# Local attention of a fused transformer: averages feature-major, two tiles projected at once, inverse norms by logarithm and exponential, another order within a period

## The chip, the cores and the metric

The kernel runs on one core of a Trainium2 chip. The metric is the device time of one execution in microseconds; the median of several runs is compared. A profiled execution gives the engine-by-engine record that the prediction works from. Engines are called as in the profile: PE (matrix products, with PEld for its weight loads), DVE (vector engine), ACT (scalar engine), POOL (GpSimd) and SP (the queue that issues most DMAs).

## The reference

Four sequences of 512 tokens with 128 features pass through four stages, each a cross-attention and a feed-forward part. The change concerns one of them only, the feed-forward part of the third stage, which is itself a transformer of six layers with local attention (16 heads of 64 features, windows of 32 tokens). Cut to what matters:

```python
def l2norm(t):
    return t / jnp.maximum(jnp.linalg.norm(t, axis=-1, keepdims=True), 1e-12)

def attn_layer(x, Wqkv, qs, ksc, Wo):
    qkv = x @ Wqkv
    q, k, v = (sh(t) for t in jnp.split(qkv, 3, -1))     # 16 heads of 64
    q = l2norm(q) * qs
    k = l2norm(k) * ksc
    q = q * cos * scale + rotate_half(q) * sin * scale
    k = k * cos * inv + rotate_half(k) * sin * inv
    # each window of 32 queries sees its own window and the one before it
    sim = jnp.einsum('bhwie,bhwje->bhwij', bq, bk2) * QK_SCALE
    sim = jnp.where(mask, -jnp.finfo(sim.dtype).max, sim)
    attn = jax.nn.softmax(sim, -1)
    out = jnp.einsum('bhwij,bhwje->bhwie', attn, bv2)
    return out.transpose(0, 2, 1, 3).reshape(b, n, INNER) @ Wo

def ffn_layer(x, g, bln, W1, b1, W2, b2):
    xn = (x - mu) / jnp.sqrt(var + 1e-05) * g + bln
    a, gate = jnp.split(xn @ W1 + b1, 2, -1)
    return a * jax.nn.gelu(gate, approximate=False) @ W2 + b2

for i in range(6):
    x = attn_layer(shift_tokens(x), Wqkv[i], q_scale[i], k_scale[i], Wo[i]) + x
    x = ffn_layer(shift_tokens(x), ln_g[i], ln_b[i], W1[i], b1[i], W2[i], b2[i]) + x
```

`shift_tokens` delays the second half of the features by one token.

## The kernel before, in words

Everything here happens in `local_transformer`. The residual stream is held feature-major in `Y[b]` (128 features by 512 tokens and one column more, so that the shift by a token is an offset of one column for partitions 64 to 127). The work on one **tile** is that on 128 tokens of one sequence in one layer: 6 layers x 4 sequences x 4 tiles = 96 tiles. A **row** is the four tiles of one sequence in one layer; its feed-forward part comes after all four.

One loop over `n` issues one **period** at a time. A period holds steps of three tiles at different ages and of one row:

- `T`, tile n: products for queries and keys (`queries_or_keys`, two halves `c` of eight heads for each `kind`: 0 queries, 1 keys), squares on ACT (L1781), the rotation on DVE (`rotate`: two products, L1789 and L1792, and the sum of squares, L1801), their sum on POOL (L1802), the inverse norms (`normalise`: a first guess by integer arithmetic on DVE, L1812 and L1813, then three Newton steps, L1817 to L1820, and the scaling, L1823, all on POOL), and the values (`values`, L1858, copied by ACT, L1859, and shifted by a window into `v2` by DMAs of SP's queue, L1861 to L1869).
- `T1`, tile n-1: queries and keys are transposed (`turned`, with `to_features`, L582; ACT copies, L1835; POOL copies the last 32 keys of the tile before in front, L1831), the scores (L1879 the mask, L1888), and the softmax up to the exponential (L1898 maximum, L1899 difference, L1904 exponential).
- `T2`, tile n-2: the probabilities are transposed (L582, ACT copies L1909), the averages (`average`, L1919), their division by the sum that a column of ones in V yields (`normalised`, L1928 and L1929), the transposition to features (`attended`, ACT copies L1938), the projection (L1943) and the residual (L1950).
- `F`, a row: its feed-forward part in four **phases**, one to a period. Phase 0: `ff_moments` early, `ff_norm` late. Phase 1: `ff_turn` early, `ff_gate` of chunks 0 and 1 (Gelu, L1981) late. Phase 2: `ff_gate` of chunk 2 early, `ff_up` (L1989, L1992) of chunks 0 and 1 late. Phase 3: `ff_up` of chunk 2 early, `ff_down` (L2001) and its residual (L1716) late. The phase of a period equals the place of T2 in its row.

There is no scheduler in this part: each engine works through its instructions in the order in which the loop issues them, and waits by semaphore for what others must have done. [...] two for `mm` (products for queries and keys), two for `tr` (all transposes, and the values), a pair `sc` (scores, and all of the feed-forward part) and a pair `av` (averages and projection).

## Time and profile before

| | |
|---|---|
| median of 3 runs | 2536.09 us (2535.72 to 2539.29) |
| profiled execution | 2544.82 us, of which the span from the first to the last instruction is 2543.0 us |
| mean granted PE clock | 0.944; 1.00 in the stretch from 700 to 2215 us |
| busy share of the span | PE 90%, PEld 59%, DVE 70%, ACT 49%, POOL 61% |
| local transformer | maximum of the softmax (L1898) 96 times, first at 568.6 us, last at 2209.6 us |
| from one maximum to the next | 17.54, 17.10, 18.39 and 15.65 us in turn where a feed-forward part runs beside; 15.17 us in the first tiles, where none does |

A row of the timeline gives the start in us, the duration, the engine, the line, the operation, what it writes and reads with its shape, how many are merged, and in brackets how long the engine was idle before and what ended that. A matmul of 32-bit floats appears as two instructions, its two passes, each with a weight load. Since the ends of matmuls are modelled, the distance from start to start is what a product costs in a stream. A group's row gives the busy total and the mean of one in ns, then the idle time of the engine before the group and its releasers. A row of waits reads: who waited for whom, us in total, times, longest. A row of a stretch gives the busy time and count for PE, PEld, DVE, ACT and POOL, then the clock, the DMA share and GB/s.

### The profile page before, as it was taken

How to read it: one execution, taken by the hardware profiler on the slowest of the kernel's cores; microseconds unless marked ns; L12 is line 12 of the kernel's file. 1: busy time of each engine (PE TensorE's matmuls, PEld its weight loads, DVE VectorE, ACT ScalarE, POOL GpSimd, SP SyncE). 2: the span in 40 equal slices, each digit the busy share in tenths (PEclk: the TensorE clock that was granted, in tenths of full speed). 3: DMA queues.
4: the chain of work that ended last, by engine and by line, in shares of the span. 5: the costliest groups of instructions: out<-in, count | busy, mean ns of one | idle time of the engine just before them, and what ended most of it. 6: DMA issues, size and time to landing. Idle time of an engine off the chain costs nothing.

```text
span 2543.0 us, 87670 instructions
## 1 busy us (share of the span) xinstructions
PE 2287.4 (90%) x37341; PEld 1489.2 (59%) x37341; DVE 1789.3 (70%) x4010; ACT 1245.4 (49%) x2186; POOL 1549.6 (61%) x2620
## 2 busy tenths in 40 slices
PE   7959879968999999999999999999999999878676
PEld 3537744536666666666666666666666666634465
DVE  5436355757888888888888888788888888646422
ACT  3523234535555555555555555555555555514232
POOL 2241232447777777777777777777777777532333
PEclk9868989979999999999999999999999999969788
DMA  6201110015311121111211121111211111102023
GB/s 160 82 20 40 37 41 2 1 49 110 105 28 34 33 61 43 32 28 34 75 28 34 34 71 34 32 28 47 60 29 34 33 27 34 28 27 58 19 70 85
DMA packets 134305, 116.21 MB, mean 46 GB/s; under 512 B 29505, under 2 KB 102700, under 8 KB 133916
## 3 DMA queue, kind: packets, MB, share of 16 engines
q1 hardware_dynamic: 128373, 102.81, 15.5%
q0 software_dynamic: 4608, 7.35, 0.9%
q8 instruction: 296, 4.85, 0.8%
q14 instruction: 93, 0.76, 0.1%
q10 hardware_dynamic: 935, 0.43, 0.1%
HBM read 42.84 MB, written 21.52 MB: 25 GB/s over the span
## 4 chain that ended last, share of the span: by engine, by line
PE 54%; DVE 24%; issue 7%; ACT 6%; POOL 4%; DMA 2%; another core or an unknown queue 1%; SPq 1%; ACTq 0%; POOLq 0%; DVEq 0%
PE ps_tr L582 8%; PE ps_mm L1779 8%; DVE rc L1789 4%; DVE rs L1792 4%; DVE ss L1801 4%; PE ps_av L1919 3%; PE ps_av L1943 3%; PE ps_tr L1858 3%; PE ps_sc L1989 3%; PE ps_sc L2001 3%; PE ps_sc L1888 2%; DVE P L1899 2%; PE ps L773 2%; DVE la_mx L1898 2%; PE ps L782 2%
## 5 line engine op out<-in xcount | busy, mean ns | idle before, releaser
L1802 POOL TENSOR_TENSOR rc<-rc,rs 128x512 f32<-128x512 f32 x384 | 488.4, 1275 | 229.3 <-DVE rs L1792 187.6
L1779 PE MATMUL ps_mm<-wqk,y 128*128 128x512 f32 x768 | 397.7, 600 | 11.0 <-DVE rs L1792 7.6
L1823 POOL TENSOR_TENSOR rc<-rc,rn_y 128x512 f32<-128x512 f32 x384 | 388.8, 1044 | 7.5
L1789 DVE TENSOR_TENSOR rc<-ps_mm,tabs 128x512 f32<-128x512 f32 x384 | 262.5, 684 | 163.0 <-ACT sq L1781 147.6
L1904 ACT ACTIVATE P<-P 128x1024 f32<-128x1024 f32 x96 | 101.5, 1057 | 419.8 <-DVE P L1899 419.8
L1781 ACT ACTIVATE sq<-ps_mm 128x512 f32<-128x512 f32 x384 | 231.0, 602 | 150.5 <-PE ps_mm L1779 103.0
L1792 DVE TENSOR_TENSOR rs<-ps_mm,tabs 128x512 f32<-128x512 f32 x384 | 261.6, 681 | 5.8 <-POOL rc L1802 5.7
L1801 DVE TENSOR_REDUCE ss<-sq 128x8 f32<-128x512 f32 x384 | 259.5, 676 | 0.0
L582 PE MATMUL ps_tr<-cst,rc 128*128 128x128 f32 x1536 | 211.4, 281 | 8.7 <-POOL rc L1823 4.5
L1919 PEld LDWEIGHTS ps_av<-v,PT 64*32 64x32 f32 x12288 | 138.0, 105 | 126.7 <-PE ps_tr L582 55.0
L1943 PE MATMUL ps_av<-aT,wo 128*128 128x128 f32 x1536 | 199.0, 282 | 4.5 <-issue 4.4
L1943 PEld LDWEIGHTS ps_av<-aT,wo 128*128 128x128 f32 x1536 | 180.8, 193 | 13.5 <-issue 4.7
L582 PEld LDWEIGHTS ps_tr<-cst,rc 128*128 128x128 f32 x1536 | 165.6, 141 | 28.7 <-POOL rc L1823 5.6
L1919 PE MATMUL ps_av<-v,PT 64*32 64x65 f32 x12288 | 169.1, 225 | 6.4 <-DVE attn L1929 5.9
L1017 POOL DMA_INDIRECT back<-ye,to x80 | 78.0, 975 | 157.5 <-DVE ye L1131 111.9
L1888 PE MATMUL ps_sc<-kT,qT 64*32 64x64 f32 x12288 | 146.4, 225 | 30.0 <-issue 22.6
L1888 PEld LDWEIGHTS ps_sc<-kT,qT 64*32 64x32 f32 x12288 | 139.8, 105 | 40.9 <-issue 27.0
L1779 PEld LDWEIGHTS ps_mm<-wqk,y 128*128 128x128 f32 x768 | 124.9, 193 | 61.0 <-issue 45.0
L763 ACT ACTIVATE P<-ps,deltaT 77x512 f32<-77x512 f32 x192 | 115.4, 683 | 73.6 <-PE ps L757 68.3
L1835 ACT COPY kT<-ps_tr 128x512 f32<-128x512 f32 x192 | 103.3, 589 | 86.1 <-PE ps_tr L582 84.9
L1835 ACT COPY qT<-ps_tr 128x512 f32<-128x512 f32 x192 | 103.2, 589 | 74.8 <-PE ps_tr L582 72.4
L1929 DVE TENSOR_TENSOR attn<-ps_av,la_den 128x512 f32<-128x512 f32 x192 | 132.8, 691 | 6.6
(392 smaller groups left out, 4510.8 us busy)
## 6 DMA issues: line engine op xcount, KB each, us to landing
v<-v SPq DMA_DIRECT2D x432, 65.0 KB
v<-v SPq DMA_DIRECT2D x96, 195.0 KB
wqk<-in_L_ffn_Wqkv_dram SPq DMA_DIRECT2D x24, 256.0 KB
sent<-xn SPq DMA_DIRECT2D x2, 2210.0 KB
xe<-sent SPq DMA_DIRECT2D x16, 260.0 KB
back<-xn SPq DMA_DIRECT2D x2, 2048.0 KB
raw<-in_L_ffn_W_dram SPq DMA_DIRECT2D x8, 512.0 KB
yb<-back SPq DMA_DIRECT2D x16, 256.0 KB
```

What stands on the lines that cost most here:

```text
L582: PE.transpose(t[:, i], src[:, i], ident)
L1779: PE.matmul(t, lhs, T.w[2 * kind + c], start=True, stop=True)
L1781: SC.activation(sq, t, AF.Square)
L1789: V.tensor_tensor(a, t, bc(T.tabs[:, 2 * kind, tt], [128, 8, LD], 1), ALU.mult)
L1792: V.tensor_tensor(r.rearrange("p h (x d) -> p h x d", x=2), t.rearrange("p h (x d) -> p h x d", x=2)[:, :, ::-1], bc(T.tabs[:, 2 * kind + ...
L1801: V.tensor_reduce(T.ss[:, kind, 8 * c : 8 * c + 8], sq, AX.X, ALU.add)
L1802: G.tensor_tensor(a, a, r, ALU.add)
L1823: G.tensor_tensor(a, a, bc(y[:, o : o + 8], [128, 8, LD], 2), ALU.mult)
L1835: SC.copy(t[:, 4 * c : 4 * c + 4, lead:], to_features(T.rot[kind, c].rearrange("p (k x) d -> p k (x d)", x=2)),)
L1888: PE.matmul(T.banks[32 * w : 32 * w + 32, z, k], T.qT[r, k, 32 * w : 32 * w + 32], T.kT[r, k, 32 * w : 32 * w + 64], start=False, stop=Tru ...
L1919: PE.matmul(T.means[32 * w : 32 * w + 32, x0, k], T.PT[r, 4 * g + k, 32 * w : 32 * w + 32], (T.v1 if w % 2 else T.v2)[r, x0, 4 * g + k], s ...
L1943: PE.matmul(t, T.wo[:, c], T.aT[:, c], start=(c == 0), stop=(c == 7))
```

## The change

- The probabilities are divided by their sums before the averages: `sums` (DVE: sum and reciprocal over the exponentials) and `shares` (POOL: two products, in place). V loses its column of ones, `normalised` goes.
- `average` takes V as the stationary operand (64 rows by 64 columns) and the transposed probabilities as the moving one (32 columns), and writes the means of all eight head pairs feature-major into the pair `av`. `attended` copies them without a transpose, into a buffer that holds two tiles.
- `project_out` and `residual` run in the periods whose T2 is the second or fourth of its row, for two tiles, 256 columns.
- `normalise` finds the inverse norms as exp(-0.5 ln(ss)) on ACT with one Newton step on POOL, which also takes the first step over from DVE. The table set that holds both functions is loaded explicitly before the loop and after the last Gelu of each row.
- The sum of `rotate` becomes a step of its own, `added`; the scaling becomes `scaled`, for queries in the same period and for keys in the next.
- The steps of a period are issued in another order.

```diff
+EXP_LN = "natural_log_exp_and_others"
...
@@ -1799,6 +1800,10 @@
                     ALU.mult,
                 )
                 V.tensor_reduce(T.ss[:, kind, 8 * c : 8 * c + 8], sq, AX.X, ALU.add)
+                T.rot[kind, c] = a, r
+
+            def added(T, kind, c):
+                a, r = T.rot[kind, c]
                 G.tensor_tensor(a, a, r, ALU.add)
                 T.rot[kind, c] = a
 
@@ -1809,18 +1814,19 @@
                 ss = T.ss.rearrange("p a b -> p (a b)")
                 y = small.tile([128, n], F32, name="rn_y")
                 t = small.tile([128, n], F32, name="rn_t")
-                V.tensor_scalar(ss, ss, 1e-24, -0.5, ALU.max, ALU.mult)
-                V.tensor_scalar(
-                    y.bitcast(I32), ss.bitcast(I32), -0.5, 0x5F3759DF - 0x40400000, ALU.mult, ALU.add
-                )
-                for _ in range(3):
-                    G.tensor_tensor(t, y, y, ALU.mult)
-                    G.tensor_tensor(t, t, ss, ALU.mult)
-                    G.tensor_scalar(t, t, 1.5, None, ALU.add)
-                    G.tensor_tensor(y, y, t, ALU.mult)
-                for (kind, c), a in sorted(T.rot.items()):
-                    o = LH * kind + 8 * c
-                    G.tensor_tensor(a, a, bc(y[:, o : o + 8], [128, 8, LD], 2), ALU.mult)
+                G.tensor_scalar(ss, ss, 1e-24, -0.5, ALU.max, ALU.mult)
+                SC.activation(y, ss, AF.Ln, scale=-2.0)
+                SC.activation(y, y, AF.Exp, scale=-0.5)
+                G.tensor_tensor(t, y, y, ALU.mult)
+                G.tensor_tensor(t, t, ss, ALU.mult)
+                G.tensor_scalar(t, t, 1.5, None, ALU.add)
+                G.tensor_tensor(y, y, t, ALU.mult)
+                T.inverse = y
+
+            def scaled(T, kind):
+                for c in range(2):
+                    a, o = T.rot[kind, c], LH * kind + 8 * c
+                    G.tensor_tensor(a, a, bc(T.inverse[:, o : o + 8], [128, 8, LD], 2), ALU.mult)
 
             def turned(T, kind):
 
@@ -1844,19 +1850,17 @@
             def values(T, x0):
 
 
-
                 b, tt = T.b, T.tt
                 if x0 == 0:
-                    T.v1 = vp.tile([128, 2, LH // 2, LD + 1], F32, name="v1")
-                    T.v2 = vp.tile([128, 2, LH // 2, LD + 1], F32, name="v2")
-                    G.memset(T.v1[:, :, :, LD : LD + 1], 1.0)
+                    T.v1 = vp.tile([128, 2, LH // 2, LD], F32, name="v1")
+                    T.v2 = vp.tile([128, 2, LH // 2, LD], F32, name="v2")
                     if tt == 0:
                         G.memset(T.v2[0:32, 0], 0.0)
                         G.memset(T.v2[64:96, 1], 0.0)
                 t = p_tr(128, 8, LD)
                 src = Y[b] if x0 == 0 else swapped[b]
                 PE.matmul(t, src[:, 128 * tt : 128 * tt + 128], T.wv[:, x0], start=True, stop=True)
-                SC.copy(T.v1[:, x0, :, 0:LD], t)
+                SC.copy(T.v1[:, x0], t)
                 if x0 == 0:
                     DMA.dma_start(T.v2[32:128, 0], T.v1[0:96, 0])
                     if tt:
@@ -1893,60 +1897,69 @@
 
             def softmax(T):
 
-                P = tp.tile([128, LH // 2, 2, LD], F32, name="P", bufs=1)
+                T.P = tp.tile([128, LH // 2, 2, LD], F32, name="P", bufs=1)
+                P = T.P.rearrange("p k z d -> p z k d")
                 mx = small.tile([128, 2, LH // 2], F32, name="la_mx")
                 V.tensor_reduce(mx, T.banks, AX.X, ALU.max)
-                V.tensor_tensor(
-                    P.rearrange("p k z d -> p z k d"), T.banks,
-                    bc(mx, [128, 2, LH // 2, LD], 3), ALU.subtract,
-                )
-                T.P = P.rearrange("p k z d -> p k (z d)")
+                V.tensor_tensor(P, T.banks, bc(mx, [128, 2, LH // 2, LD], 3), ALU.subtract)
                 SC.activation(T.P, T.P, AF.Exp, scale=8.0)
+
+            def sums(T):
+                T.sum = small.tile([128, LH // 2, 2], F32, name="la_sum")
+                V.tensor_reduce(T.sum, T.P, AX.X, ALU.add)
+                V.reciprocal(T.sum, T.sum)
+
+            def shares(T):
+
+                for g in range(2):
+                    k = slice(4 * g, 4 * g + 4)
+                    P = T.P[:, k].rearrange("p k z d -> p (k z) d")
+                    rec = T.sum[:, k].rearrange("p k z -> p (k z)")
+                    G.tensor_tensor(P, P, bc(rec, [128, 8, LD], 2), ALU.mult)
 
             def probabilities(T):
                 T.PT = tp.tile([128, LH // 2, 128], F32, name="PT", bufs=1)
+                P = T.P.rearrange("p k z d -> p k (z d)")
                 for g in range(2):
-                    SC.copy(T.PT[:, 4 * g : 4 * g + 4], to_features(T.P[:, 4 * g : 4 * g + 4]))
-
-            def average(T, g):
-                if g == 0:
-                    T.attn = tp.tile([128, LH // 2, 2, LD], F32, name="attn", bufs=1)
-                T.means = pair("av")[:, :, : 4 * LD + 4].rearrange("p x (k d) -> p x k d", d=LD + 1)
-                for k in range(4):
+                    SC.copy(T.PT[:, 4 * g : 4 * g + 4], to_features(P[:, 4 * g : 4 * g + 4]))
+
+            def average(T):
+
+
+                t = pair("av").rearrange("p s (k q) -> p s k q", q=64)
+                for k in range(LH // 2):
                     for w in range(4):
                         for x0 in range(2):
                             r = slice(64 * (x0 ^ (w // 2)), 64 * (x0 ^ (w // 2)) + 64)
+                            q = 32 * (w % 2)
                             PE.matmul(
-                                T.means[32 * w : 32 * w + 32, x0, k],
-                                T.PT[r, 4 * g + k, 32 * w : 32 * w + 32],
-                                (T.v1 if w % 2 else T.v2)[r, x0, 4 * g + k],
-                                start=True, stop=True,
+                                t[64 * x0 : 64 * x0 + 64, w // 2, k, q : q + 32],
+                                (T.v1 if w % 2 else T.v2)[r, x0, k],
+                                T.PT[r, k, 32 * w : 32 * w + 32], start=True, stop=True,
                             )
-
-            def normalised(T, g):
-                den = small.tile([128, 2, 4], F32, name="la_den")
-                V.reciprocal(den, T.means[:, :, :, LD])
-                V.tensor_tensor(
-                    T.attn[:, 4 * g : 4 * g + 4].rearrange("p k x d -> p x k d"),
-                    T.means[:, :, :, 0:LD], bc(den, [128, 2, 4, LD], 3), ALU.mult,
-                )
+                T.means = t
 
             def attended(T):
-                flat = T.attn.rearrange("p k x d -> p k (x d)")
-                T.aT = tp.tile([128, LH // 2, 128], F32, name="aT", bufs=1)
-                for g in range(2):
-                    SC.copy(T.aT[:, 4 * g : 4 * g + 4], to_features(flat[:, 4 * g : 4 * g + 4]))
+
+                if T.tt % 2 == 0:
+                    T.aT = tp.tile([128, LH // 2, 256], F32, name="aT", bufs=1)
+                else:
+                    T.aT = T.before.aT
+                for s in range(2):
+                    o = 128 * (T.tt % 2) + 64 * s
+                    SC.copy(T.aT[:, :, o : o + 64], T.means[:, s])
 
             def project_out(T):
-                t = pair("av")[:, 0, :128]
+
+                t = pair("av")[:, 0, :256]
                 for c in range(8):
                     PE.matmul(t, T.wo[:, c], T.aT[:, c], start=(c == 0), stop=(c == 7))
                 T.out = t
 
             def residual(T):
-                t = T.out
-                for r, o in ((slice(0, 64), 0), (slice(64, 128), 1)):
-                    dst = Y[T.b][r, 128 * T.tt + o : 128 * T.tt + o + 128]
+                t, o0 = T.out, 128 * (T.tt - 1)
+                for r, o in ((slice(0, 64), o0), (slice(64, 128), o0 + 1)):
+                    dst = Y[T.b][r, o : o + 256]
                     V.tensor_tensor(dst, t[r], dst, ALU.add)
 
 
@@ -2020,6 +2033,7 @@
                     ff_up(F, 0, 1)
                 elif phase == 2:
                     ff_gate(F, 2)
+                    SC.preload_act_table_set(EXP_LN)
                 elif phase == 3:
                     ff_down(F) if second else ff_up(F, 2)
 
@@ -2030,6 +2044,7 @@
             loaded = {0: load(0)}
             tabs = {0: tables(loaded[0][5])}
             swap(0)
+            SC.preload_act_table_set(EXP_LN)
             for n in range(len(tiles) + 10):
                 T = tiles[n] if n < len(tiles) else None
                 T1 = tiles[n - 1] if 0 <= n - 1 < len(tiles) else None
@@ -2051,32 +2066,36 @@
                     T.tabs = tabs[T.i]
                     queries_or_keys(T, 0, 0)
                 if T2:
-                    probabilities(T2)
+                    sums(T2)
                 if T:
                     queries_or_keys(T, 0, 1)
                     rotate(T, 0, 0)
+                if T1:
+                    scaled(T1, 1)
+                if T2:
+                    shares(T2)
+                if T1:
+                    turned(T1, 0)
                 if F:
                     ff_stage(F, phase, False)
-                if T2:
-                    average(T2, 0)
-                if T1:
-                    turned(T1, 0)
                 if T:
+                    added(T, 0, 0)
                     queries_or_keys(T, 1, 0)
-                if T2:
-                    normalised(T2, 0)
-                if T:
                     rotate(T, 0, 1)
-                if T2:
-                    average(T2, 1)
+                    added(T, 0, 1)
                 if T1:
                     turned(T1, 1)
+                if T2:
+                    probabilities(T2)
                 if T:
+                    rotate(T, 1, 0)
+                    added(T, 1, 0)
                     queries_or_keys(T, 1, 1)
                 if T2:
-                    normalised(T2, 1)
+                    average(T2)
                 if T:
-                    rotate(T, 1, 0)
+                    rotate(T, 1, 1)
+                    added(T, 1, 1)
                 if T2:
                     attended(T2)
                 if T and T.tt == NT - 1 and n + 1 < len(tiles):
@@ -2084,12 +2103,11 @@
                 if T1:
                     scores(T1)
                 if T:
-                    rotate(T, 1, 1)
-                if T:
                     normalise(T)
+                    scaled(T, 0)
                 if T1:
                     softmax(T1)
-                if T2:
+                if T2 and T2.tt % 2:
                     project_out(T2)
                     residual(T2)
                 if F and phase == 0:
```

## The prediction

> **What bounds the kernel now.** I read the page's first two parts, then busy time by stretch, the totals of waits, the groups, and last the timeline of one engine at a time. The local transformer owns two thirds of the span: the first maximum of its softmax (L1898) starts at 568.6 us and the last at 2209.6. The page and a stretch inside it:
>
> ```profile
> PE 2287.4 (90%) x37341; PEld 1489.2 (59%) x37341; DVE 1789.3 (70%) x4010; ACT 1245.4 (49%) x2186; POOL 1549.6 (61%) x2620
> ```
>
> ```profile
> 1100.00:1500.00 400.00, 384.68 (x7740) 257.93 (x7739) 332.15 (x612) 227.62 (x391) 308.56 (x538) 1.00 0.14 38
> ```
>
> PE shows 96% busy at clock 1.00, but its ends are modelled, so I count starts. Without feed-forward work a tile needs 14.13 us of PE (602.25 to 616.4, start to start), yet L1898 comes every 15.17 us there (568.56, 583.66, 598.83, 614.00). So PE is not the first bound. The waits say what is:
>
> ```profile
> ACT P L1904 <- DVE P L1899: 419.8, 96, 6.0
> POOL rc L1802 <- DVE rs L1792: 187.6, 244, 6.0
> DVE rc L1789 <- ACT sq L1781: 147.6, 54, 5.7
> ```
>
> DVE and ACT wait for each other in a ring. One turn, from phase 1 to phase 2 of a row, on DVE and then on ACT:
>
> ```profile
> 1431.54 1.22 DVE L1898 TENSOR_REDUCE la_mx<-ps_sc 128x16 f32<-128x1024 f32 x1
> 1432.79 1.23 DVE L1899 TENSOR_TENSOR P<-ps_sc,la_mx 128x1024 f32<-128x1024 f32 x1
> ...
> 1439.17 0.69 DVE L1789 TENSOR_TENSOR rc<-ps_mm,tabs 128x512 f32<-128x512 f32 x1 [4.65 <-ACT sq L1781]
> ```
>
> ```profile
> 1434.05 1.06 ACT L1904 ACTIVATE P<-P 128x1024 f32<-128x1024 f32 x1 [4.10 <-DVE P L1899]
> 1435.02 1.06 ACT L1859 COPY v<-ps_tr 128x512 f32<-128x512 f32 x2
> 1436.09 1.28 ACT L1981 ACT_TABLE_LOAD   x1
> 1437.38 1.27 ACT L1981 ACTIVATE fh<-ps_sc,cols 128x512 f32<-128x512 f32 x2
> 1438.54 0.60 ACT L1781 ACTIVATE sq<-ps_mm 128x512 f32<-128x512 f32 x1
> ```
>
> Maximum, difference, exponential, V copies, in this phase table and Gelu, then the squares that the first rotation waits for. From 1439.17 DVE is solid to the next maximum at 1449.08: four rotations of 1.80, two normalisations of 0.83, 1.0 for L1812 and L1813. The intervals between maxima repeat as 17.54, 17.10, 18.39, 15.65: **68.68 us a row** of four tiles, in which PE has 4 x 14.13 + 8.85 of feed-forward = 65.4.
>
> [...] 105 ns at 32 columns and 193 at 128 is 0.92 ns a column. [...] the trace has 1283 ns for each switch and two switches a row, and keeps two.
>
> **Part by part, per tile.**
>
> ```profile
> L1802 POOL TENSOR_TENSOR rc<-rc,rs 128x512 f32<-128x512 f32 x384 | 488.4, 1275 | 229.3 <-DVE rs L1792 187.6 <-PE ps_tr L582 36.1 <-PE ps_sc L1956 2.0
> L1823 POOL TENSOR_TENSOR rc<-rc,rn_y 128x512 f32<-128x512 f32 x384 | 388.8, 1044 | 7.5
> L1919 PEld LDWEIGHTS ps_av<-v,PT 64*32 64x32 f32 x12288 | 138.0, 105 | 126.7 <-PE ps_tr L582 55.0 <-PE ps_mm L1779 22.1 <-ACT PT L1909 21.3
> L1943 PEld LDWEIGHTS ps_av<-aT,wo 128*128 128x128 f32 x1536 | 180.8, 193 | 13.5 <-issue 4.7
> ```
>
> - DVE: out go two L1929 and L1928 (1.66) and L1812, L1813 (1.0). In come a sum over 1024 elements (1.25, as L1898) and a reciprocal (0.2). The residual, four 64x128 per two tiles at 0.285, becomes two 64x256 (0.42, as L2110): -0.15. Net -1.35.
> - POOL: twelve Newton steps (4.1) become five (1.7); dividing P adds two of L1823's form (2.0); a memset goes (0.1). Net -0.5, but POOL now waits for Ln and Exp on ACT: 128x32, 0.23 each as L917, with hand-overs 0.65. Net about zero.
> - ACT: +0.46 for these two, in a queue 57% busy. The copies stay 512 wide.
> - PE: 8 transposes of the average go (0.97 with the mode change behind them, of which 0.1 returns between average and scores). The projection was 16 passes at 118 ns (1.89); two tiles together take 16 passes of 256, 0.216 each by half of a 512 pass (0.43), 3.46 for two: -0.16.
> - The average stays 128 passes, moving 32 columns instead of 65, loading 64 instead of 32. Today they start 10.2 ns apart (64 in 0.65 us). **No trace row has 64x64**: below, today's pace, 1.3 us; [...] I take 1.7 plus 0.1 drain; today 1.6 plus 0.3 drains.
>
> PE's own work falls to 13.1 a tile, 61.3 a row. Memsets of v2, V's DMAs (65 columns to 64) and their SP queue keep their places; the averages read V two periods later, and that distance hides them, so I cost them at nothing; were it gone, the four issues of about 0.56 us on SP's queue, 2.2 us a tile.
>
> **The walk.** Work is not the bound, so I lay the new order out engine by engine, in order, with these durations; hand-overs from the timeline: PE start to ACT 1.11 (a 512 product), squares to rotation 0.63, rotation to POOL's sum 1.42. Zero is the first product of phase 0.
>
> Phase 0: DVE still has the residual of ff_down (to 1.74), and now `sums` before the first rotation: 3.2 instead of 1.75. POOL divides P 3.3 to 5.3, then stands at the feed-forward's inverse deviation, now queued before `added`; it needs the moments (6.07) and ends 7.5. Behind it wait two sums and the kT head, to 10.4, for which scores wait: 10.5 to 12.15. Maximum 12.35, difference to 14.85, exponential 15.95, V copies, squares, next rotation 17.45. PE's phase ends at 13.9 for 11.9 of work. POOL ends Ln, Exp, Newton and `scaled` of queries at 17.3.
>
> Phase 1: so turning the queries waits until 17.4 (PE was free 15.6), POOL scales keys to 19.3 and divides P to 21.35; probabilities are turned 21.4, fourth product, average 23.25, scores 25.05, the double projection 26.7 to 30.15, values 31.9. V copies, table and Gelu lie behind values: squares 35.15, rotation 35.8. PE's phase ends 33.6.
>
> Phase 2: the preload follows Gelu in ACT's queue (38.0 to 39.3). Squares, kT and PT copies stand behind it; the two transpose banks are full, and PE turns probabilities only from 40.35. Average 42.3, scores 44.1 to 45.75. No projection covers the softmax here, so ff_up waits for the score banks until 48.45; DVE gets both chunks at 50.45 and ends 51.85.
>
> Phase 3: `sums` to 53.3, rotation, ff_up's chunk, rotation; probabilities 57.8, average 58.75, scores 60.55, projection 62.2, values 65.65, ff_down 67.4 to **70.0**.
>
> A row is 70.0 against 68.68, the gain of the DVE ring being spent on POOL's longer queue, the preload and two bunched projections: +1.3 x 24 = +32 us. About 7 tiles without feed-forward gain 0.85 each (POOL near 14.3 against 15.17): -6. New tables every layer (3 us on POOL) cost as now. Sum +26 on the profiled execution's 2544.8 (span 2543.0), 2570.8; the median of the runs is 8.7 lower: **2562 us**.
>
> **Rivals.**
> 1. *Faster: POOL and the preload do not hold PE.* Place: turning queries and probabilities in phases 1 and 2. If the waits there vanish, PE's 61.3 plus the 3.3 a row that it loses today is 64.6: -4.1 x 24 - 6 = -104, 2432 us. For it: POOL waits 229 us today before L1802, room for dividing; the DVE ring is 2 us shorter. Against: dividing sits ahead of the sums in an ordered queue. It decides once probabilities are turned within about 0.5 us of PE being free; half the effect, and an average at today's pace (-0.4 in three phases, -29 us), give 2485. I expect 2430 to 2530.
> 2. *Much slower: the average's loads are not hidden.* 20 ns a pass, +0.9 in phases 1, 2 and 3: +65, 2627 us. [...] Against: 128-column passes of L773 start four at a time every 110 ns, with no room for a load in turn.
> 3. *No change:* 2536, if gains and waits cancel. That the new normalisation changes nothing by itself, POOL net zero, speaks for it.
>
> **Chances.** Under 0.2% (5 us) no measurement of this kernel tells. The walk 0.43, own range 2545 to 2605 (0.6 us a row and the average between its lower bound and mine); rival 2 0.15; rival 1 0.36; rival 3 0.06. Slower 0.58, same 0.06, faster 0.36. The range 2470 to 2630 leaves out the lower part of rival 1 and the tail of rival 2, 0.2 together.
>
> **What would show it.** In the changed profile: no L1929 form and fewer transposes; averages of 128 passes in 1.7 us; ACT waiting for POOL before Ln; PE's transposes of P waiting for POOL in phase 1 and for ACT's copies in phase 2; ff_up's product waiting for DVE's difference; intervals of maxima near 14.5, 19, 16.5 and 20. I am wrong if the sum of four falls under 67, or if PE starts its average without such waits; and in size if the average takes under 1.4 or over 2.3.

## The result, and the profile after

The changed kernel takes **2834.71 us** in the median of 4 runs (2825.08 to 2851.57), the kernel before beside it 2537.50 (4 runs). The ratio is 1.117, with a 95% interval of 1.114 to 1.121: slower by 297 us, where 26 were forecast. The profiled execution took 2828.35 us, with a span of 2826.6.

The page's engine line and the row of the same stretch as before (busy time of PE, PEld, DVE, ACT, POOL, each with its count, then clock, DMA share, GB/s):

```profile
PE 2280.1 (81%) x35805; PEld 1462.2 (52%) x35805; DVE 1691.9 (60%) x3530; ACT 1299.4 (46%) x2379; POOL 1566.6 (55%) x2044
```

```profile
1100.00:1500.00 400.00, 327.49 (x6244) 214.90 (x6237) 259.36 (x417) 203.29 (x371) 269.24 (x348) 0.99 0.13 33
```

All five engines lost share in the stretch (PE 384.7 to 327.5, DVE 332.2 to 259.4). No engine has become a bound by its work; each now waits for others. The local part, first to last maximum, went from 1641.1 us to 1936.6: 295.5 us, nearly all of the difference. The totals of waits name the place (waiting engine and line, the one it waits for: us, times, longest). After:

```profile
DVE la_mx L1903 <- PE ps_sc L1892: 334.3, 96, 13.3
...
POOL P L1918 <- DVE la_sum L1910: 310.9, 77, 18.7
...
PEld ps_sc L1892 <- issue: 172.0, 97, 4.8
...
PE ps_sc L1892 <- issue: 156.6, 96, 4.6
...
PEld ps_mm L1780 <- DVE rs L1793: 138.6, 95, 8.9
...
PE ps_av L1935 <- issue: 27.6, 33, 5.8
```

And the rows of before that answer to the third and the first:

```profile
PEld ps_sc L1888 <- issue: 27.0, 27, 1.5
...
DVE la_mx L1898 <- PE ps_sc L1888: 3.9, 3, 3.0
```

Before, the maximum waited for scores in 3 tiles of 96, 3.9 us in all. Now it does in every tile, 334.3 us. The scores' weight loads stood 27.0 us without a releaser ("issue"), now 172.0. And PE's products for queries and keys wait 95 times for a rotation, 94 of them the third product of a tile; before, they did so 3 times. POOL, which the prediction made the narrow place, waits for DVE's sums.

The chain of waits through one tile (start, us, what). It is read downwards; each line was released by the one above:

```profile
1382.56 0.61 DVE rs L1793
1383.21 1.14 PE ps_mm L1780 x2
1384.43 0.60 ACT sq L1782
1385.03 0.48 ACT kT L1841
1385.64 1.12 PE ps_tr L583 x8
1386.76 0.86 PE ps_mm L1780 x2
1387.62 1.98 PE ps_av L1935 x119
1389.60 0.71 issue
1390.31 0.42 PE ps_av L1935 x9
1391.08 1.12 PE ps_sc L1892 x76
1392.20 1.58 issue
1393.78 0.43 PE ps_sc L1892 x17
1394.24 1.24 DVE la_mx L1903
```

A rotation frees one of the two PSUM buffers `mm` for the third product; then follow the key copy, the transposes of P, the fourth product, average, scores, maximum, and from there the sums and the next rotation. It is a closed ring: in the same trace the rotation after this maximum ends at 1401.1 us, and the next third product starts at 1401.17. Of one turn 11 us run on PE and ACT, while DVE has only three rotations and, in this phase, the statistics of a layer norm left to do. DVE shows the end of them and the gap:

```profile
1389.93 0.68 DVE L1802 TENSOR_REDUCE ss<-sq 128x8 f32<-128x512 f32 x1
1394.24 1.22 DVE L1903 TENSOR_REDUCE la_mx<-ps_sc 128x16 f32<-128x1024 f32 x1 [3.63 <-PE ps_sc L1892]
```

Two lines of that chain are "issue": the profile shows nothing that PE waited for, and yet it did nothing. PE's timeline of the same tile shows where:

```profile
1387.55 2.05 PE L1935 MATMUL ps_av<-PT,v 64*64 64x32 f32 x119
1390.31 0.42 PE L1935 MATMUL ps_av<-PT,v 64*64 64x32 f32 x9 [0.71 <-issue]
1390.67 0.41 PE L1883 MATMUL ps_sc<-maskw,identb 64*32 64x512 bf16 x8
1390.89 1.31 PE L1892 MATMUL ps_sc<-kT,qT 64*32 64x64 f32 x111
1393.78 0.35 PE L1892 MATMUL ps_sc<-kT,qT 64*32 64x64 f32 x17 [1.58 <-issue]
```

From stall to stall there are 9 + 8 + 111 = 128 passes, with their weight loads 256 instructions. The block stalls twice, each time by more than 0.4 us, in 30 of the 96 tiles, and in all 30 the distance is exactly 128 passes. The page's row of the instruction queue (packets, MB, share) fits that:

```profile
q8 instruction: 284, 4.65, 0.7%
```

4.65 MB in 284 packets is 16.4 kB a packet. How much of PE's work goes with one is shown by the runs: the kernel with half of the average, below, has 12,288 fewer instructions on PE and PEld (2 x 29,661 against 2 x 35,805) and 48 fewer packets (236), the kernel before 3,072 more (2 x 37,341) and 12 more packets (296). That is 256 instructions a packet both times, 64 bytes each, and 256 is the distance of the stalls. In the dense stretch above two such transfers start at 1387.30 and 1391.44 us, 4.1 us apart; in the whole trace no two start less than 3.2 us apart (theory F, below, puts this at 3.4), and nine in ten of the stalls end 1.2 to 1.6 us after one has landed. Average, mask and scores are 264 passes (64 averaging and 64 score calls in fp32, two passes each, and 8 mask calls in bf16, one each) in one block that takes 3.7 us where nothing stalls, so 128 of its passes need some 2 us or less. All this fits PE running out of instructions in the block, which no trace shows directly; the kernel with the values in between, below, tests it. Summed over the distances above 0.25 us from the start of one weight load to the next inside scores and averages, the stalls are 218 us now and 32 before.

### The profile page after: what moved, and what is told of

The parts are those of the page before. It is cut to its first block, busy times and chain, and to the rows that moved or that the text cites. A ratio compares the mean times of both kernels' runs of the same rounds, so it can differ in the third digit from the quotient of the medians.

```text
span 2826.6 us, 83266 instructions
## 1 busy us (share of the span) xinstructions
PE 2280.1 (81%) x35805; PEld 1462.2 (52%) x35805; DVE 1691.9 (60%) x3530; ACT 1299.4 (46%) x2379; POOL 1566.6 (55%) x2044
## 3 DMA queue, kind: packets, MB, share of 16 engines
q8 instruction: 284, 4.65, 0.7%
## 4 chain that ended last, share of the span: by engine, by line
PE 54%; DVE 22%; issue 11%; ACT 9%; DMA 2%; POOL 2%; SPq 1%; another core or an unknown queue 0%; POOLq 0%; ACTq 0%; DVEq 0%
PE ps_av L1935 7%; PE ps_av L1956 7%; PE ps_sc L1892 5%; PE ps_mm L1780 4%; PE ps_tr L1862 4%; PE ps_tr L583 4%; DVE rc L1790 3%; DVE la_sum L1909 3%; ACT sq L1782 2%; PE ps_sc L2014 2%; DVE rs L1793 2%; DVE xn L523 2%; PE ps_sc L2002 2%; DVE la_mx L1903 2%; DVE fh L2005 2%
## 5 line engine op out<-in xcount | busy, mean ns | idle before, releaser
L1918 POOL TENSOR_TENSOR P<-P,la_sum 128x512 f32<-128x512 f32 x192 | 196.4, 1044 | 340.8 <-DVE la_sum L1910 310.9
L1903 DVE TENSOR_REDUCE la_mx<-ps_sc 128x16 f32<-128x1024 f32 x96 | 117.6, 1225 | 334.3 <-PE ps_sc L1892 334.3
L1892 PE MATMUL ps_sc<-kT,qT 64*32 64x64 f32 x12288 | 166.5, 226 | 157.3 <-issue 156.6
L1935 PEld LDWEIGHTS ps_av<-PT,v 64*64 64x64 f32 x12288 | 199.5, 135 | 102.8 <-ACT PT L1924 72.0
L583 PEld LDWEIGHTS ps_tr<-cst,rc 128*128 128x128 f32 x1536 | 178.2, 141 | 128.4 <-issue 95.4
L1892 PEld LDWEIGHTS ps_sc<-kT,qT 64*32 64x32 f32 x12288 | 148.0, 106 | 177.6 <-issue 172.0
L1935 PE MATMUL ps_av<-PT,v 64*64 64x32 f32 x12288 | 214.1, 221 | 28.2 <-issue 27.6
L583 PE MATMUL ps_tr<-cst,rc 128*128 128x128 f32 x1536 | 201.9, 274 | 18.0 <-ACT v L1863 13.3
L1956 PE MATMUL ps_av<-aT,wo 128*128 128x256 f32 x768 | 187.1, 399 | 1.2 <-ACT aT L1950 1.2
L1950 ACT COPY aT<-ps_av 128x512 f32<-128x512 f32 x192 | 103.1, 589 | 176.4 <-PE ps_av L1935 176.4
L1956 PEld LDWEIGHTS ps_av<-aT,wo 128*128 128x128 f32 x768 | 148.0, 198 | 25.7 <-ACT aT L1950 1.3
L583 PE MATMUL ps_tr<-cst,P 128*128 128x128 f32 x768 | 108.3, 281 | 63.3 <-ACT kT L1841 62.7
```

The lines of the kernel that those rows point to most:

```text
L583: PE.transpose(t[:, i], src[:, i], ident)
L1892: PE.matmul(T.banks[32 * w : 32 * w + 32, z, k], T.qT[r, k, 32 * w : 32 * w + 32], T.kT[r, k, 32 * w : 32 * w + 64], start=False, stop=Tru ...
L1918: G.tensor_tensor(P, P, bc(rec, [128, 8, LD], 2), ALU.mult)
L1935: PE.matmul(t[64 * x0 : 64 * x0 + 64, w // 2, k, q : q + 32], (T.v1 if w % 2 else T.v2)[r, x0, k], T.PT[r, k, 32 * w : 32 * w + 32], start ...
L1956: PE.matmul(t, T.wo[:, c], T.aT[:, c], start=(c == 0), stop=(c == 7))
```

## The experiments

The partial kernels ran on chips where the kernel before takes 2489 to 2499 us, because the stages outside the local part are shorter there. So ratios are compared, and a forecast in us, made for a kernel before of 2536, has to be read as a difference. The changed kernel was measured there too:

> The changed kernel once more, so that the partial kernels have it beside them on one chip, where the kernel before takes 2489 us because its first stage ends 38 us earlier. If the local transformer's part is the same as in the first comparison (1936.6 us between the first and the last maximum), this takes 2796 us, ratio 1.123.

Measured: 2794.16 us, ratio 1.119 (1.116 to 1.122). The local part took 1943.1 us; the first maximum came 27 us earlier than in the first comparison, and what follows the last was 16 us shorter.

In the expectations, F and S stand for the supply of instructions, Q for the order of POOL's and VectorE's work, R for the ring, P for TensorE's own work.

**The parts alone.** The kernel before with only the new norms:

```
-                V.tensor_scalar(ss, ss, 1e-24, -0.5, ALU.max, ALU.mult)
...
+                SC.activation(y, ss, AF.Ln, scale=-2.0)
+                SC.activation(y, y, AF.Exp, scale=-0.5)
...
```

> The kernel before with the inverse norms by logarithm and exponential alone (with the table set loaded after the last Gelu). Ring theory: L1812 and L1813 leave DVE's turn, 1.0 us a tile, POOL has 1.7 less after the wait for ACT: 2536 falls by 60 to 95, to 2440 to 2476 us. Rival: the preload inside ACT's queue in phase 2 and the hand-over POOL, ACT, POOL take it back: 2515 to 2545 us.

Measured: 2452.53 us, ratio **0.984** (0.982 to 0.986). This beats both kernels, but the fall of 37 us lies between the two forecasts, 60 to 95 and 21 at most. The kernel before with only the two-tile projection:

```
...
-                if T2:
+                if T2 and T2.tt % 2:
                     project_out(T2)
                     residual(T2)
```

> The kernel before with the projection and residual of two tiles at once alone. PE's own work falls by 0.16 us a tile, but a 3.5 us projection stands ahead of values and ff_down in the second and fourth tile of a row. Bunching theory: odd intervals get 1.6 us longer, even ones gain at most as much as DVE's ring allows, 2540 to 2575 us. Rival, work theory: 2515 to 2530 us.

Measured: 2570.56 us, ratio 1.032 (1.029 to 1.034). That is 81 us more, twice the upper end of the bunching theory (4 to 39). The work is no more, but 3.6 us of it stand in each second tile. The rest, the average with the new order, is the changed kernel without these two:

```
-                SC.activation(y, ss, AF.Ln, scale=-2.0)
...
-                if T2 and T2.tt % 2:
+                if T2:
...
```

> The changed kernel without two of its parts: the projection of one tile in each period, and the inverse norms by the bit trick and three Newton steps, both as in the kernel before. What is left of the change is the feature-major average and the new order. If the parts add (norms alone 0.984, projection alone 1.032), these two alone make nearly all of it: 1.10 to 1.13. If the parts only cost together, by filling the same gaps, it is under 1.06.

Measured: 2786.41 us, ratio 1.113 (1.109 to 1.117). The parts add up to 12.9% against 11.9% measured together, so the average with its order carries the loss. Taken out of the changed kernel one at a time, first the two-tile projection:

```
...
-                t = pair("av")[:, 0, :256]
+                t = pair("av")[:, 0, :128]
...
```

> The changed kernel, with the output projection and its residual of one tile in each period (128 columns) instead of two tiles in each second one. Nothing is left out. The kernel before with only the two-tile projection lost 3.2%. If that cost stands in the changed kernel too, the ratio falls from 1.117 to about 1.085 (1.07 to 1.10), with the four intervals of the maximum nearer to each other. If the instruction supply covers it (the even tiles without a projection are the ones that wait for instructions, and eight more matmuls come into each of them), there is no change: 1.11 to 1.13, stalls in scores and average still near 218 us.

Measured: 1.108 (1.106 to 1.111), between the two forecasts: a gain of 1.1 points where 3.2% alone was measured; the maximum still waits 323.7 us for scores. Then the norms:

```
-                SC.activation(y, ss, AF.Ln, scale=-2.0)
...
+                for _ in range(3):
+                    G.tensor_tensor(t, y, y, ALU.mult)
...
```

> The changed kernel, with the inverse norms by the bit trick and three Newton steps as in the kernel before, and without the table loads for logarithm and exponential. Nothing is left out. With the norms alone the kernel before gained 1.6%. If that gain is in the changed kernel too, this one is slower than it: ratio 1.13 to 1.14. If PE's wait for instructions sets the end in the changed kernel, the norms are hidden: 1.11 to 1.125.

Measured: 1.130 (1.127 to 1.133). The norms gain about 1% inside the changed kernel too; they are not hidden by the other losses.

**Stalls, or the place?** Half of the average left out:

```
-                for k in range(LH // 2):
+                for k in range(LH // 4):
...
```

> The changed kernel with the averages of four of the eight head pairs alone (the copies take each of them twice, so all other work is as it was; half of the averages is left out). PE's own work falls by 1.0 us a tile, 96 us in all. Theory F: [...] the issue gaps of 1.9 us a tile go too: 2834 falls to 2540 to 2620 us. Theory Q: 96 us or less, 2740 to 2800 us.

Measured: 2590.81 us, ratio 1.041 (1.037 to 1.044). The local part fell by 191 us, where 96 times half an average (1.0 us) and 110 us of stalls (218 to 108) make 206. That is twice what theory Q allows, and a little short of theory F, which also had all stalls gone: half of them stayed. The wait of the maximum:

```profile
DVE la_mx L1903 <- PE ps_sc L1892: 131.9, 87, 12.0
```

So what is taken out in front of the scores counts about one to one. But this removes passes and stalls together. The next kernel takes out no pass and aims at the stalls, with value products in their place:

```
                 if T2:
                     attended(T2)
+                if T:
+                    values(T, 0)
+                    values(T, 1)
                 if T and T.tt == NT - 1 and n + 1 < len(tiles):
                     swap(tiles[n + 1].b)
                 if T1:
                     scores(T1)
...
```

> The changed kernel, with the two value matmuls of the next tile (512 columns each, 1.1 us of work in 2 to 4 instructions) issued between the average and the scores instead of behind the scores. Nothing is left out. Theory F (instruction supply): the 264 passes of average, mask and scores no longer stand in one block; a block of 1.1 us with hardly an instruction lies between them and lets a chunk arrive, so the stalls inside scores and average fall from 218 us to 90 to 140 us, and the ratio to the kernel before from 1.117 to 1.05 to 1.09. Theory Q (the order of POOL's and VectorE's work is what is late, the stalls are slack): the stalls may fall but the maximum still waits for the same thing, ratio 1.10 to 1.125. Against both: the values' copies go to ScalarE ahead of the exponential.

Measured: 2793.18 us, ratio 1.122 (1.120 to 1.124). The stalls did go, from 218 us to 48, more than theory F had foretold. Its waits:

```profile
DVE la_mx L1903 <- PE ps_sc L1892: 356.5, 96, 12.3
...
PE ps_sc L1892 <- issue: 10.6, 14, 1.5
```

```profile
1424.11 2.09 PE L1935 MATMUL ps_av<-PT,v 64*64 64x32 f32 x128
1426.13 1.12 PE L1862 MATMUL ps_tr<-wv,y 128*128 128x512 f32 x2
1427.09 1.02 PE L1862 MATMUL ps_tr<-wv,yw 128*128 128x512 f32 x2
1428.04 0.41 PE L1883 MATMUL ps_sc<-maskw,identb 64*32 64x512 bf16 x8
1428.27 1.64 PE L1892 MATMUL ps_sc<-kT,qT 64*32 64x64 f32 x128
```

Scores wait 10.6 us without a releaser instead of 156.6, and the kernel is no faster: in each tile 1.9 us of value products now stand where 1.8 us of stalls had stood, in front of the scores on the same ring. One thing blurs this: PE's clock in the local part was 0.94 here against 0.98 in the changed kernel beside it. The three rows of this kernel at 0.98 took 80.5 us, eight such rows of the changed kernel 82.1, so at the same clock the edit may gain some 1.5 us a row, 36 us in 24 rows (an estimate). Even so the ratio would be about 1.107, short of the 1.05 to 1.09 of the supply theory. It was a miss of that theory as it was put, and it gave the better one: **the stalls cost because of where they lie.** With the single projection as well:

> The changed kernel with both of the edits above: the values' matmuls between average and scores, and the projection of one tile in each period. Nothing is left out. If the two causes add, the ratio is 1.02 to 1.06; if each covers the other, it is near the better of the two alone. Theory Q: 1.08 to 1.12.

Measured: 1.097 (1.095 to 1.099), outside the forecast for two causes that add; the place is still untouched. Against the single projection alone (1.108), at the same clock of 0.97 to 0.98 in the local part, the values in between gain 1.1 points, 31 us, for about 130 us of stalls that go (177 to 45).

The other way round, the average behind the scores:

```
-                if T2:
-                    average(T2)
...
-                if T2:
-                    attended(T2)
...
                 if T1:
                     softmax(T1)
+                if T:
+                    values(T, 0)
+                    values(T, 1)
+                if T2:
+                    average(T2)
+                    attended(T2)
                 if T2 and T2.tt % 2:
                     project_out(T2)
...
```

> The changed kernel, with scores issued right after the fourth product, then the softmax and the values, and only then averages, their copies, projection and residual: average and scores no longer stand side by side on PE. Theory F (PE runs out of instructions: its instruction chunks of 16 KB, 128 passes with their weight loads, arrive every 3.4 us or later, while average and scores use 128 passes in 2 us): the idle time that ends in 'issue' inside these two falls from 1.9 us a tile to under 0.5, a row of four maxima from 80.6 us to 70 to 74, the time to 2600 to 2680 us. Theory Q (the waits come from the order of the queues of POOL and ACT, as in the walk, and the issue gaps only fill time in which PE would wait anyway): a row of 78 to 81, 2770 to 2840 us.

Measured: 2714.7 us, ratio 1.090 (1.087 to 1.093). The stalls fall to 43 us, as theory F said, but a row still takes 79.2, as theory Q said. The wait of the maximum falls to 15.8 us, and another takes its place, on DVE and on PE:

```profile
1362.98 0.86 DVE L1963 TENSOR_TENSOR y<-ps_av,y 64x256 f32<-64x256 f32 x2 [6.83 <-PE ps_av L1956]
```

```profile
1359.22 3.72 PE L1956 MATMUL ps_av<-aT,wo 128*128 128x256 f32 x16 [1.34 <-ACT aT L1950]
```

The residual stands first in DVE's queue, for a projection that now ends late, and the sums and rotations stand behind it: 371.5 us of waits in 48 tiles. So projection and residual were moved into the next period:

```
                 if T1:
                     turned(T1, 0)
+                if T3 and T3.tt % 2:
+                    project_out(T3)
+                    residual(T3)
...
```

> The changed kernel with another order, nothing left out: scores, softmax and values as soon as the fourth product is issued, average and its copies behind the values, and the projection of two tiles with its residual in the next period, behind the turned queries. Theory R (the ring: maximum, sums, rotations, third and fourth product, average, scores, maximum; what stands between the fourth product and the scores counts one to one, the average with 2.0 us and the stalls in average and scores with 1.9 us a tile): the block in front of the maximum is 3.9 us shorter, the residual that held VectorE 7 to 8 us in the kernel with scores first is gone, VectorE's or TensorE's own work of 62 to 68 us a row is the next bound: a row takes 66 to 72 us against 80.5, ratio 0.98 to 1.04, and VectorE waits for scores under 120 us instead of 334. Theory S (supply alone, wherever the passes stand: the number of instructions is the same): stalls only move to the average, ratio 1.07 to 1.10.

Measured: 2592.64 us, ratio **1.038** (1.035 to 1.040), and with the projection of one tile in each period:

> The same order as the kernel with the later projection, with the projection and residual of one tile in each period. Nothing is left out. Theory R: the double projection of 3.6 us stands in each second period beside the other work and makes the periods uneven, as in the kernel before with it alone (3.2%): this one is 0 to 3% faster than the kernel with two tiles, ratio 0.97 to 1.03. Theory S: the 8 more matmuls a row count little, 1.06 to 1.10.

2538.58 us, ratio **1.016** (1.014 to 1.018). The maximum's wait in the first and the second:

```profile
DVE la_mx L1903 <- PE ps_sc L1892: 14.3, 10, 6.2
```

```profile
DVE la_mx L1903 <- PE ps_sc L1892: 8.2, 6, 6.3
```

And PE's timeline of the second, with the same 64 average and 64 score calls as in the changed kernel:

```profile
1422.66 0.41 PE L1883 MATMUL ps_sc<-maskw,identb 64*32 64x512 bf16 x8
1422.89 1.46 PE L1892 MATMUL ps_sc<-kT,qT 64*32 64x64 f32 x128
1424.28 1.12 PE L1862 MATMUL ps_tr<-wv,y 128*128 128x512 f32 x2
1425.24 1.02 PE L1862 MATMUL ps_tr<-wv,yw 128*128 128x512 f32 x2
1426.19 2.09 PE L1935 MATMUL ps_av<-PT,v 64*64 64x32 f32 x128
```

One change of order, of the average and of the projection behind it, takes 8.1 of the 11.9 points back, and the single projection 2.2 more. The stalls are 48 and 33 us now. No kernel here takes the stalls alone out of the ring; this one moves the average and loses the stalls at once. The block in front of the maximum is shorter by 15.6 us a row (four times 3.9), and the row by 8.0, so what binds then is something else. The ring theory's row of 66 to 72 us for the first was missed by 1.6 us (73.6); the second has 71.8. (These are means over the rows; by the same count the changed kernel has 81.6 and the kernel before 69.4.)

**What holds the better order now?** It is still slower than the kernel before with the new norms (68.2 us a row). Two guesses at ScalarE's queue. The copies of the average behind the squares:

```
                 if T:
                     queries_or_keys(T, 0, 1)
+                if T3:
+                    attended(T3)
...
```

> The order with the later projection of one tile, and ScalarE's two copies of the average (1.08 us together) moved too: they stand behind the first two squares of the next period instead of ahead of them. Nothing is left out. Theory R (the ring through ScalarE: difference, exponential, V copies, aT copies, squares, first rotation): the copies come off the ring, a row takes 67.5 to 70.5 us instead of 71.8, ratio 0.97 to 1.00. Theory P (TensorE's own work of some 62 to 65 us a row with its small waits is the bound now): 1.01 to 1.02, no change; the projection then also waits for the later copies.

Measured: 2623.31 us, ratio 1.053 (1.051 to 1.054), slower by 3.7 points, which neither theory had. PE's projection now waits for the copies in 94 tiles, and the residual behind it (128.9 us, before 23.6):

```profile
1400.77 2.05 PE L1952 MATMUL ps_av<-aT,wo 128*128 128x128 f32 x16 [0.78 <-ACT aT L1946]
```

Then the first product and its square ahead of the values, in that kernel and in the kernel before with the new norms:

```
+            def begin(n):
+                T = tiles[n]
...
+                queries_or_keys(T, 0, 0)
...
+                if n + 1 < len(tiles):
+                    begin(n + 1)
                 if T:
                     values(T, 0)
```

> The same, and the first product of the next tile with its square is issued ahead of the values, so that ScalarE's square of it lies ahead of the two V copies (1.06 us) and of a Gelu with its table load. Nothing is left out. Theory R: up to another 1.06 us a tile and 2.5 in one phase come off the ring, a row of 63 to 68 us, ratio 0.93 to 0.98. Theory P: like the kernel without it within 1%.

> The kernel before with only the inverse norms by logarithm and exponential (0.984 of the kernel before), and the first product of the next tile with its square issued ahead of the values, so that ScalarE squares before it copies V. Nothing is left out. Theory R: VectorE's first rotation starts about 1 us earlier in each tile, a row takes 64.5 to 67 us instead of 68.2, ratio 0.945 to 0.975. Theory P (TensorE has 65.4 us of its own in a row and waits for few): 0.975 to 0.99.

Measured: 1.051 (1.049 to 1.053) and 0.992 (0.990 to 0.993). The first is what theory P had, the second is outside both. So both guesses at ScalarE's queue fell, and the second edit lost 0.75% to the kernel without it. DVE's waits there, first without the edit and then, in two lines, with it:

```profile
DVE rc L1790 <- ACT sq L1782: 125.2, 31, 5.5
```

```profile
DVE la_den L1927 <- PE ps_av L1918: 97.9, 30, 6.2
...
DVE rc L1790 <- ACT sq L1782: 41.2, 31, 5.0
```

84 us of the wait for squares went (125.2 to 41.2), and 86 came for the average on PE (11.8 to 97.9). With 65.4 us of its own work in a row of 68.2, as the prediction counts it, PE may be the next bound behind the ring. What exactly holds the better order at 71.8 us was not settled.

## Why the prediction was wrong

- **The direction was right, the mechanism mostly not**, so the direction was in good part luck. Slower was forecast for POOL's longer queue, the preload and bunched projections. POOL waits 310.9 us for sums, so dividing P does not bind. Of the waits foretold, P's transposes wait in nearly every tile, but 0.43 us for the key copies, not for POOL; in phase 2 they wait 1.35 behind the preload, as the walk had it, and `ff_up` waits for the difference. ACT waits for POOL before the logarithm in 75 tiles, as foretold (48.4 us), and POOL longer for ACT behind it (71.9).
- **"The walk" is the step that failed.** It set the queue in the right order (fourth product, average, scores, maximum), but gave each block its passes' own time. Average and scores stand still for 218 us, 2.3 us a tile, against 32 before, and in this order that lies on the ring. The intervals of the maxima, foretold as 14.5, 19, 16.5 and 20 us, came as 17.2, 23.0, 18.4 and 23.0: in the foretold order, and too long by 2.7, 4.0, 1.9 and 3.0. PE's idle time inside average, mask and scores, 1.6, 3.0, 1.2 and 2.0 us in the four, goes with that. If the stalls count in full, which the half average makes likely (191 of 206 us) and no kernel shows alone, these 186 us are the largest part of the 270 that were missing. The sign was in the trace of before: 27 us of "issue" in the loads of the scores at a block half as long, which the walk left unpriced.
- **The same step took the order itself as nearly free.** The walk's row of 70.0 against 68.68 says that an average between the fourth product and the scores costs next to nothing (in the kernel before, both of its halves stood ahead of that product). Moving it behind them, and the projection with it into the next period, is worth 202 us (2794.16 to 2592.64), in which the stalls are contained.
- **The average's 1.8 us was a little small.** Without a stall it takes 2.02 (1424.11 to 1426.13 in the timeline of the values in between), within the bounds given. Its 1.7 us, 13.3 ns a pass, was the author's estimate, and so was Rival 2's 20 ns: no trace of before shows a 64x64 pass. Measured were 15.8 ns, over 96 tiles 21 us more than the walk has; Rival 2 did not happen. What the prediction calls drain and mode change is time between PE's blocks in the trace of before: 64 averaging passes, 10.2 ns apart, take 0.79 us to the start of the next transposes (1425.04 to 1425.83), 0.14 more than at that pace; eight transposes take 0.97 us ahead of the mask (1427.62 to 1428.59) and 0.87 ahead of a product (603.11 to 603.98). The 0.92 ns a column of the prediction is a slope alone: the loads recorded at 105, 135 and 193 ns with 32, 64 and 128 columns (L1919 and L1943 before, L1935 after) have some 76 ns beside it, and the transposes' loads of 128 columns (L582) take 141 ns.
- **The projection was mis-sized.** It was walked into a row that lost 1.3 us for all reasons; by itself it costs 3.2%, and 1.1 and 2.2 points in two orders of the new kernel. The larger period is not given back by the smaller one.
- **Norms at "net zero" were wrong the other way**: −1.6% alone. The 1.0 us of DVE that they free counts by 0.4 a tile (37 us over 96). ACT loads tables as often as before, two of 1283 ns a row (48 loads, before 47), none of them between logarithm and exponential.
- **Rival 1 assumed that with POOL and the preload out of the way PE's work sets the end.** The opposite happened: PE's share fell, and the chain above has it in series with DVE. (The 2485 there is not the sum of the terms beside it: 2536 less 52 and 29 is 2455. Nothing hangs on it.)
- What stays open: stalls (186) and the average's size (21) leave about 65 of the missing 270 us unassigned between projection, key copies and hand-overs. Some of it goes with PE's clock, 0.98 in the local part against 1.00 before: the eleven rows of the changed kernel at a clock of 1.00 took 80.8 us against 81.6 in the mean, which would be 18 us in 24 rows (an estimate).

## What to carry to other kernels

When an edit moves a block of work to another place in an in-order queue, ask first which engine waits for what stands behind it, and whether that engine feeds the queue again: on such a ring it counted nearly one to one here (191 us of 206) until something else bound, elsewhere the same block cost far less (202 us less, its stalls included). Count instructions too, not only their time: here a run of 264 tiny passes, 528 instructions with their loads, stood still for 2.3 us a tile, and two long products between its halves took the stalls from 218 us to 48. Such products are worth a try between two runs, but not in front of what is waited for: there the kernel was no faster (ratio 1.122). Try the parts of a combined change alone; here one of three was the gain.

## What was not expected of the hardware

- In the changed kernel PE stalled at exact distances of 128 passes (256 instructions) in the 30 tiles with two stalls, mostly 0.8 to 2.1 us each, with no open wait in the profile; transfers of 16.4 kB on the instruction queue never started less than 3.2 us apart, and 4.1 us apart in the block shown. Two value products of 512 columns between two dense blocks (1.9 us) removed 93% of the stalls in the second block (156.6 to 10.6 us).
- A 64x64-tile pass of 32 columns in fp32, weight load included, starts every 15.8 ns (2.02 us for 128), although in the records each load takes 135 ns and each pass 221:

```profile
L1935 PE MATMUL ps_av<-PT,v 64*64 64x32 f32 x12288 | 214.1, 221 | 28.2 <-issue 27.6
L1935 PEld LDWEIGHTS ps_av<-PT,v 64*64 64x64 f32 x12288 | 199.5, 135 | 102.8 <-ACT PT L1924 72.0
```
